# Receptance by seven products in one slot of four, states times std, the second norm's sums on ScalarE, and the next unit's attention first in a slot

## The chip, the cores and the metric

The kernel runs on one core of one Trainium2 chip, in float32 throughout. The metric is the device time of one execution in microseconds. In the text PE is TensorE, DVE is VectorE, ACT is ScalarE, POOL is GpSimd, and SP is the engine that issues most DMAs.

## What is computed

One transformer-like layer on x of 4 batches x 2048 tokens x 512 features. The parts that matter, cut from the reference (M = 64; `_layernorm` subtracts the mean and divides by the root of variance + 1e-5):

```python
h = _layernorm(x) * (1 + ca) + sa
x = x + ga * attention(h)
h = _layernorm(x) * (1 + cb) + sb
x = x + gb * ffn(h)

# attention(u): gates omega, zeta and F are products of u with 64 + 64 + 128 columns, then a scan over tokens
z_new = d_t * (S_t * z - DT * A_t * S_t * y) ; y_new = d_t * (DT * S_t * z + S_t * y) ; state = [z_new, y_new] + F_t
y = einsum('btn,dn->btd', states, C) + einsum('bte,de->btd', u, D_mat)

# ffn(x): x_prev is x moved by one token
xr = mu_r * x + (1 - mu_r) * x_prev ; xk = mu_k * x + (1 - mu_k) * x_prev
r = sigmoid(xr @ W_r.T) ; k = square(relu(xk @ W_k.T)) ; out = r * (k @ W_v.T)
```

The factors sa, ca, ga, sb, cb, gb come per batch from a small product of silu(c).

## The kernel before

**Tiling.** A unit is 256 tokens (W) of one batch: two tiles of 128 tokens (NT = 2). There are 32 units; unit i belongs to block s = i // 4 and batch b = i % 4. All matmuls are float32; a contraction over 512 features is 4 steps of 128. The norm's scale is folded into the weights: D's product runs on raw x with weights `dg` scaled per batch, and its result is multiplied by the token's r = 1/std afterwards.

**Classes.** `Gates` (`gts[j]`) makes a unit's scan inputs: `load`, `norm` (ACT sums with accumulators, L181 and L183, then POOL's power, L188), `send` (r to DRAM, L192), `spread` (r back as a row on all partitions, `bc`, L200), `project` (PE, tile `pg`, L221), `multiply` (DVE, L227), `deliver` (ACT, L242). `scan(s)` returns the DVE steps of a block's scan, each with an estimated cost in us; they go into the list `side`, and `take(budget)` runs steps from it until the budget is used up. Its last step `by_batch` copies the states on ACT (L377) and sends them to tile `y` by eight DMAs (L380). A `None` in the list is passed over by the next `take`.

`Finish` (`fin[i]`) does the rest of a unit. `attend` makes D's product `pd` (L424, 4 matmuls per tile), C's product `pc` (L449, one matmul), adds both to x on DVE (L430 and L463), takes bn_stats for the second norm (L125, L126), POOL powers (L471, L472), and the normalised `xn` on ACT (L475). `mix` transposes xn on PE (`pt`, L494) and forms the two mixtures with the previous token by ACT and DVE (L500, L503), with the key's sums (L546 to L549) between. `shift` adds a row to the next x on POOL (L417). `key_fast` computes the 512 x 512 x 256 product of W_k by Strassen's scheme in Winograd's form: seven products of halves, 28 matmuls of 128 columns (L562) in four rounds into two PSUM tiles `pm`, added up by DVE (L570 to L580), then Relu and Square on ACT (L583, L518). `receptance` is the plain product: 8 matmuls of 512 columns (L592), Sigmoid from PSUM (L594). `value` makes `pv` (L607), multiplies by r and adds x on DVE (L610, L611), and sends the rows out (L613).

**Order.** Every engine runs its instructions in the order in which the code gives them; the schedule is written by hand (`manual_schedule`). The loop at L1029 has one pass ("slot") per unit. For i >= 4, with at = i % 4:

```python
f.key_fast()
norm_send(i + 9)
take(a); ahead.attend(lambda: take(a2)); fetch("dg", i + 3); take(b_)
f.receptance()
ahead.mix(...); load_t, spread of unit i + 9; gates(i + 8)
f.value(lambda: take(c)); fetch("wv", i + 2)
```

where `ahead` is unit i + 1. The budgets are fixed for at = 0, 1; at = 2 takes shares of what is left; at = 3 starts with `take(100)`, and puts the next block's scan into `side` at its end, so it has no scan steps of its own. The first four slots have their own order. Before the loop a long set-up (L683 to L1006) makes weights per batch and runs block 0's scan.

PSUM pools: `ps1` one buffer (`pg`), `ps2` two buffers each of `pm` and `pt`, `ps3` three of `px`. SBUF pools p1, p2, p3 have one, two, three buffers per tag; the tag `soft` is in p1.

Of the kernel before, what the change touches and what calls it, by code (L numbers as in the profile page):

```python
# [21 lines left out]
P = 128  # L22
# [25 lines left out]
def adaln_layer_kernel(ctx: ExitStack, tc: tile.TileContext, x, x_t, c_t, wmod, w_gate, w_b, b_gate, b_f, c_mat, d_mat,  # L48
# [28 lines left out]
    rs = const.tile([P, B, T // P], F32, name="rs")  # L77
# [18 lines left out]
    pmean = const.tile([P, KC, 2 * B], F32, name="pmean")  # L96
# [51 lines left out]
    class Gates:  # L148


        def __init__(self, unit):
            self.u = unit
            self.r = rs[:, unit.b, unit.t0 // P : unit.t0 // P + NT]
# [8 lines left out]
        def norm_dve(self):  # L162
            tag = self.u.tag
            mv = p2.tile([P, NT, 2], F32, tag="mv", name=f"mv_a{tag}")
            for n in range(NT):
                tile_stats(self.xs[n], mv[:, n, :], f"a{tag}_{n}")
            var = p2.tile([P, NT], F32, tag="var", name=f"var_{tag}")
            nc.vector.tensor_scalar_add(var, mv[:, :, 1], EPS)
            nc.gpsimd.tensor_tensor(self.r, var, neg_half, ALU.pow)

        def norm(self, junk=False):
# [16 lines left out]
            nc.gpsimd.tensor_tensor(self.r, var, neg_half, ALU.pow)  # L188

        def send(self, queue=nc.sync):  # L190
            self.row = dram.tile([W], F32, tag=f"st{self.u.tag}", name=f"st_{self.u.tag}")
            queue.dma_start(self.row.rearrange("(n p) -> p n", p=P), self.r)  # L192
# [5 lines left out]
        def spread(self, queue=nc.sync):  # L198
            self.bc = p2.tile([P, W], F32, tag="bc", name=f"bc_{self.u.tag}")
            queue.dma_start(self.bc, self.row.unsqueeze(0).broadcast_to([P, W]))  # L200
# [43 lines left out]
    def scan(s):  # L244
# [125 lines left out]

        def by_batch():

            y_of[s] = p2.tile([P, B, W], F32, tag="y", name=f"y_{s}")
            for q in range(Q):
                t = [pre[:, i].rearrange("p l q c -> p (l q c)")[:, ts(q, W)] for i in range(2)]
                for i in range(2):
                    nc.scalar.copy(t[i].rearrange("p (c l) -> p l c", l=L), f[:, i, :, q, :])  # L377
                for r in range(2):
                    for i in range(2):
                        nc.sync.dma_start(y_of[s][ts(i, M), 2 * q + r, :], t[i][ts(r, M), :])  # L380
# [6 lines left out]
            + [(fall_start, 0.8)]  # L387
# [3 lines left out]
        return [(soften_act, 0), None] + steps + [None, (by_batch, 0)]  # L391

    class Finish:


        def __init__(self, unit):
            self.u, self.tag = unit, f"c{unit.tag}"


            self.fast = unit.s > 0  # L400
            self.at = unit.i % 2 if self.fast else unit.b
# [17 lines left out]
        def direct(self, n, room=(ps3, "px")):  # L419

            u = self.u
            pd = room[0].tile([P, D], F32, tag=room[1], name=f"pd_{self.tag}_{n}")
            for k in range(KC):
                nc.tensor.matmul(pd, self.h[:, k, ts(n, P)], dg[:, self.at, k, :], start=(k == 0), stop=(k == KC - 1))  # L424
            return pd

        def add_direct(self, n, pd):
            u, xt = self.u, self.x[:, n, :]
            r = rs[:, u.b, u.t0 // P + n : u.t0 // P + n + 1]
            nc.vector.scalar_tensor_tensor(xt, pd, r, xt, ALU.mult, ALU.add)  # L430
# [11 lines left out]
        def rows(self, n):  # L442

            return ps3.tile([P, D], F32, tag="px", name=f"pc_{self.tag}_{n}")

        def states(self, n, pc):

            u = self.u
            nc.tensor.matmul(pc, y_of[u.s][:, u.b, ts(n, P)], cg[:, u.b, :], start=True, stop=True)  # L449

        def attend(self, between):
            xt = self.x
            mv = p2.tile([P, NT, 2], F32, tag="mv", name=f"mv_{self.tag}")
            pcs = None
            if self.pd is not None:
                pcs = [self.rows(n) for n in range(NT)]
            for n in range(NT):
                pd = self.direct(n) if self.pd is None else None
                pc = pcs[n] if pcs else self.rows(n)
                self.states(n, pc)  # L460
                if pd is not None:
                    self.add_direct(n, pd)
                nc.vector.tensor_add(xt[:, n, :], xt[:, n, :], pc)  # L463
                tile_stats(xt[:, n, :], mv[:, n, :], f"{self.tag}_{n}")
                if n == 0:
                    between()
            rstd = p2.tile([P, NT], F32, tag="rstd", name=f"rstd_{self.tag}")
            nmr = p2.tile([P, NT], F32, tag="nmr", name=f"nmr_{self.tag}")
            nc.vector.tensor_scalar_add(rstd, mv[:, :, 1], EPS)
            nc.vector.tensor_scalar_mul(nmr, mv[:, :, 0], -1.0)  # L470
            nc.gpsimd.tensor_tensor(rstd, rstd, neg_half, ALU.pow)  # L471
            nc.gpsimd.tensor_tensor(nmr, nmr, rstd, ALU.mult)  # L472
            self.xn = p1.tile([P, NT, D], F32, tag="xn", name=f"xn_{self.tag}")
            for n in range(NT):
                nc.scalar.activation(  # L475
                    self.xn[:, n, :], xt[:, n, :], AF.Identity, bias=nmr[:, n : n + 1], scale=rstd[:, n : n + 1]
# [63 lines left out]
        def key_sums(self):  # L540
            (b00, b01), (b10, b11) = self.quarters = [
                [self.mixed[:, 1, 2 * k : 2 * k + 2, ts(t, P)] for t in range(2)] for k in range(2)
            ]
            half = dg[:, 3].rearrange("p k d -> p (k d)")[:, ts(self.u.i % 2, 2 * D)]
            t = self.sums = half.rearrange("p (i k w) -> p i k w", i=4, k=2)
            nc.vector.tensor_sub(t[:, 0], b01, b00)  # L546
            nc.vector.tensor_sub(t[:, 1], b11, t[:, 0])
            nc.vector.tensor_sub(t[:, 2], b11, b01)
            nc.vector.tensor_sub(t[:, 3], b10, t[:, 1])  # L549

        def key_fast(self):
            (b00, b01), (b10, b11) = self.quarters
            t, s = self.sums, key_weights
            act = self.act = p1.tile([P, KC, W], F32, tag="act", name=f"act_{self.tag}")
            (c00, c01), (c10, c11) = [[act[:, 2 * o : 2 * o + 2, ts(h, P)] for h in range(2)] for o in range(2)]

            def products(*pairs):
                pk = ps2.tile([P, 2, 2, P], F32, tag="pm", name=f"pk_{self.tag}")
                for n, (left, right) in enumerate(pairs):
                    for j in range(2):  # L560
                        for k in range(2):
                            nc.tensor.matmul(  # L562
                                pk[:, n, j, :], left[:, k, ts(j, P)], right[:, k, :], start=(k == 0), stop=(k == 1)
                            )
                return pk[:, 0], pk[:, 1]

            add = nc.vector.tensor_add
            x1, x2 = products((wk[:, 0:2, : D // 2], b00), (wk[:, 2:4, : D // 2], b10))
            copy = nc.scalar.copy if self.u.b else nc.vector.tensor_copy
# [5 lines left out]
            x7, x3 = products((s[:, 2], t[:, 2]), (s[:, 3], b11))  # L575
# [3 lines left out]
            x4, _ = products((wk[:, 2:4, D // 2 :], t[:, 3]))  # L579
            add(c10, c10, x4)  # L580
            for e in range(KC // 2):
                a = self.act[:, 2 * e : 2 * e + 2, :]
                nc.scalar.activation(a, a, AF.Relu)  # L583
                self.squares(e)

# [31 lines left out]
    key_weights = dg[:, 2].rearrange("p k d -> p (k d)").rearrange("p (i k o) -> p i k o", i=4, k=2)  # L617

    def make_key_weights():
        s = key_weights  # L620
        (a00, a01), (a10, a11) = [
            [wk[:, 2 * k : 2 * k + 2, ts(o, D // 2)] for k in range(2)] for o in range(2)
        ]
# [3 lines left out]
        nc.vector.tensor_sub(s[:, 3], a01, s[:, 1])  # L627

# [116 lines left out]

    def gate_cols(dst, pt, name):

        raw, sgn = (const.tile([P, KC, B], F32, name=f"{kind}{name}") for kind in ("raw", "sgn"))
# [114 lines left out]
    means = shared_means()  # L863
    gts[0].diagonal(cg[:, 0, :W])
# [5 lines left out]
    shared_weights(1, pws[0])  # L870
    gts[1].diagonal(cg[:, 1, :W])
# [6 lines left out]
    pws = [shared_product(3, means)]  # L878
    gts[2].diagonal(cg[:, 2, :W])
# [11 lines left out]
    for i in range(2):  # L891
        for k in range(KC):
            nc.tensor.matmul(pb[:, i, :], wraw[:, k, i, :], mod[:, SA, k, :], start=(k == 0), stop=(k == KC - 1))
    gts[3].diagonal(cg[:, 3, :W])
# [91 lines left out]
    d_scaled(2, pcas[0])  # L986
# [3 lines left out]
    fin[0].attend(lambda: None)  # L990
    d_scaled(3, pcas[1])
# [36 lines left out]

    for i, f in enumerate(fin):  # L1029
        at = i % B  # L1030
        ahead = fin[i + 1] if i + 1 < len(fin) else None
        if i < 4:
# [15 lines left out]
            if i == 2:  # L1048
                make_key_weights()
            ahead.attend(lambda: take(2))  # L1050
            turn(turn_v[i])
# [29 lines left out]
        else:  # L1081
# [6 lines left out]
            f.key_fast()  # L1088
            if i + 9 < len(gts):
                norm_send(i + 9)  # L1090
            if at == B - 2:
                left = sum(e[1] for e in side if e)
                a, a2, b_, c = 0.33 * left, 0.11 * left, 0.45 * left, 0.11 * left
            else:
                a, a2, b_, c = (3.6, 1.2, 5.5, 1.2) if at else (3.0, 0.0, 7.0, 1.2)
            take(a)
            if ahead:
                ahead.attend(lambda: take(a2))
            fetch("dg", i + 3)
            take(b_)  # L1100
            f.receptance()
# [56 lines left out]
```

## Time and profile before

| what | value |
|---|---|
| median of 3 runs (lowest, highest) | 1152.9 us (1152.21, 1157.6) |
| the profiled execution's own time | 1154.13 us |
| its span on the core | 1152.4 us |
| mean granted PE clock | 0.985 |
| DMA, mean over the span | 144 GB/s, queue 1 at 54.6% of 16 engines |
| receptance, L592 | 256 matmuls of 512 columns in 512 records, 227.6 us busy |
| DVE addition of C's product, L463 | 64, 687 ns each |
| DVE bn_stats L125, bn_aggr L126 | 64 of 695 ns, 64 of 182 ns |
| ACT copies of states, L377 | 32, 676 ns each |

The rows of the groups give line, engine, operation and tiles with partitions x elements, then the total busy time in us and the mean in ns of one, then the engine's idle time just before them and what ended it. Matmuls overlap, so the time that one takes is read from start to start. PEld is the weight load, which runs beside the matmul. In timelines a row is a run of like instructions: start, duration from the first start to the last end, and how many; a bracket tells of idle time before them.

### The profile page before, as it was taken

The numbers are of one execution on the slowest core, as the hardware profiler recorded it, in microseconds if no ns is written. First come the engines' busy times: TensorE is split into PE (matmuls) and PEld (weight loads), VectorE is DVE, ScalarE is ACT, GpSimd is POOL, SyncE is SP. The second block draws the span as 40 slices with busy tenths as digits, with TensorE's granted clock in tenths as the row PEclk, the third lists the DMA queues.
The fourth block names the chain that finished last, engine by engine and source line by source line (L and its number), as shares of the span: only waits on it lengthen the run. The fifth ranks groups of instructions, "written<-read, shape, count | busy, mean of one in ns | idle before, by whom it ended". The sixth has DMA issues, their size and how long they took to land.

```text
span 1152.4 us, 14032 instructions
## 1 busy us (share of the span) xinstructions
PE 1119.8 (97%) x4460; PEld 680.9 (59%) x4460; DVE 819.1 (71%) x2251; ACT 560.4 (49%) x1055; POOL 165.9 (14%) x317
## 2 busy tenths in 40 slices
PE   7899999999999999999999999999999999999998
PEld 4556566665565666655656666566566645555555
DVE  5897778458884787748886588847876588855553
ACT  1655775755535654455435644546444533333331
POOL 0222101111101111111011111110111111111110
PEclk8889899999999999999999999999999999999999
DMA  9893363445676656567667665676564423343211
GB/s 319 285 194 112 95 188 111 151 159 89 159 160 170 136 161 159 93 174 160 157 132 196 151 143 123 141 178 140 146 149 127 143 79 118 119 146 128 92 55 37
DMA packets 125601, 166.38 MB, mean 144 GB/s; under 512 B 15700, under 2 KB 88404, under 8 KB 117720
## 3 DMA queue, kind: packets, MB, share of 16 engines
q1 hardware_dynamic: 122520, 164.17, 54.6%
q10 hardware_dynamic: 2688, 0.79, 0.3%
q0 software_dynamic: 320, 0.53, 0.3%
q8 instruction: 35, 0.57, 0.2%
q14 instruction: 38, 0.31, 0.1%
HBM read 136.07 MB, written 25.20 MB: 140 GB/s over the span
## 4 chain that ended last, share of the span: by engine, by line
PE 81%; DVE 11%; ACT 3%; DMA 2%; issue 1%; POOL 1%; DVEq 0%; POOLq 0%; ACTq 0%
PE pv_c L607 17%; PE pd_c L424 15%; PE pr_c L592 15%; PE pk_c L562 14%; PE pg L221 9%; PE pc_c L449 4%; PE pt_c L494 2%; PE pk_c L527 2%; DVE x L463 1%; DVE stats_c L125 1%; DMA bc<-st 1%; DMA st<-rs 1%; DVE uv L365 1%; PE turn_d L814 1%; DVE x L430 1%
## 5 line engine op out<-in xcount | busy, mean ns | idle before, releaser
L424 PE MATMUL pd_c<-dg,xt 128*128 128x512 f32 x512 | 232.2, 597 | 0.0
L592 PE MATMUL pr_c<-wr,mixed_c 128*128 128x512 f32 x512 | 227.6, 598 | 0.4 <-DVE act_c L578 0.4
L607 PE MATMUL pv_c<-wvb,act_c 128*128 128x512 f32 (+1 forms) x528 | 225.5, 580 | 1.1 <-DVE r_c L610 1.1
L503 DVE SCALAR_TENSOR_TENSOR mixed_c<-pt_c,prev_f,mixed_c 128x255 f32<-128x255 f32 x256 | 115.9, 479 | 91.1 <-ACT mixed_c L500 88.4
L592 PEld LDWEIGHTS pr_c<-wr,mixed_c 128*128 128x128 f32 x512 | 98.0, 192 | 122.3 <-issue 120.1
L475 ACT ACTIVATE xn_c<-x,nmr_c,rstd_c 128x512 f32<-128x512 f32 x64 | 48.6, 806 | 244.5 <-POOL nmr_c L472 244.5
L607 PEld LDWEIGHTS pv_c<-wvb,act_c 128*128 128x128 f32 x528 | 99.3, 190 | 107.9 <-issue 102.8
L424 PEld LDWEIGHTS pd_c<-dg,xt 128*128 128x128 f32 x512 | 96.0, 192 | 108.7 <-issue 107.6
L500 ACT ACTIVATE mixed_c<-pt_c,mod,now_f 128x256 f32<-128x256 f32 x256 | 130.4, 561 | 56.2 <-DVE mixed_c L503 52.6
L221 PE MATMUL pg<-xt,wgb 128*128 128x256 f32 x448 | 102.6, 383 | 0.0
L583 ACT ACTIVATE act_c<-act_c 128x512 f32<-128x512 f32 x56 | 34.8, 621 | 115.2 <-DVE act_c L578 115.2
L221 PEld LDWEIGHTS pg<-xt,wgb 128*128 128x128 f32 x448 | 84.1, 193 | 10.6
L430 DVE SCALAR_TENSOR_TENSOR x<-pd_c,rs,x 128x512 f32<-128x512 f32 x64 | 47.2, 738 | 59.0 <-PE pd_c L424 59.0
L562 PE MATMUL pk_c<-dg 128*128 128x128 f32 x672 | 79.9, 275 | 1.4 <-DVE r_c L610 1.4
L562 PEld LDWEIGHTS pk_c<-dg 128*128 128x128 f32 x672 | 77.3, 192 | 1.8 <-DVE r_c L610 1.8
L610 DVE TENSOR_TENSOR r_c<-pv_c,r_c 128x512 f32<-128x512 f32 (+1 forms) x66 | 44.2, 669 | 40.4 <-PE pv_c L607 31.7
L417 POOL TENSOR_TENSOR x<-x,d 128x1024 f32<-128x1024 f32 x30 | 70.8, 2360 | 0.0
L449 PE MATMUL pc_c<-cg,y 128*128 128x512 f32 x128 | 65.0, 592 | 0.0
L471 POOL TENSOR_TENSOR rstd_c<-rstd_c,neg_half 128x2 f32<-128x2 f32 x32 | 25.4, 793 | 272.6 <-DVE nmr_c L470 272.6
L562 PEld LDWEIGHTS pk_c<-mixed_c,wk 128*128 128x128 f32 x448 | 53.8, 192 | 16.4 <-issue 10.2
L242 ACT ACTIVATE pre<-g,bias 64x256 f32<-64x256 f32 x56 | 41.6, 743 | 36.0 <-DVE g L227 29.2
L562 PE MATMUL pk_c<-mixed_c,wk 128*128 128x128 f32 x448 | 55.0, 276 | 1.6 <-POOL mixed_c L506 1.6
(218 smaller groups left out, 1467.8 us busy)
## 6 DMA issues: line engine op xcount, KB each, us to landing
dg<-dg SPq DMA_DIRECT2D x30, 1024.0 KB, 12.2
xt<-in_x_t_dram SPq DMA_DIRECT2D x116, 256.0 KB, 7.2
wvb<-wv SPq DMA_DIRECT2D x26, 1024.0 KB, 5.2
x<-in_x_dram SPq DMA_DIRECT2D x32, 512.0 KB, 6.2
out_dram<-r_c SPq DMA_DIRECT2D x62, 256.0 KB, 2.1
xs<-in_x_dram SPq DMA_DIRECT2D x54, 256.0 KB, 6.3
wvb<-in_wmod_dram SPq DMA_DIRECT2D x5, 1024.0 KB, 9.0
y<-pre SPq DMA_DIRECT2D x64, 64.0 KB, 2.0
```

The lines of the kernel that those rows point to most:

```text
L221: nc.tensor.matmul(self.pg[:, i, :], wgb[:, b, k, ts(i, P)], self.xt[:, k, :], start=(k == 0), stop=(k == KC - 1))
L417: engine.tensor_tensor(xt, xt, d0[:, self.u.b, :].unsqueeze(1).broadcast_to([P, NT, D]), ALU.add)
L424: nc.tensor.matmul(pd, self.h[:, k, ts(n, P)], dg[:, self.at, k, :], start=(k == 0), stop=(k == KC - 1))
L430: nc.vector.scalar_tensor_tensor(xt, pd, r, xt, ALU.mult, ALU.add)
L449: nc.tensor.matmul(pc, y_of[u.s][:, u.b, ts(n, P)], cg[:, u.b, :], start=True, stop=True)
L475: nc.scalar.activation(self.xn[:, n, :], xt[:, n, :], AF.Identity, bias=nmr[:, n : n + 1], scale=rstd[:, n : n + 1])
L500: nc.scalar.activation(m, pt, AF.Identity, bias=mod[:, SB, k, b : b + 1], scale=now_f[:, b, i, k : k + 1])
L503: nc.vector.scalar_tensor_tensor(m[:, 1:], pt[:, : W - 1], prev_f[:, b, i, k : k + 1], m[:, 1:], ALU.mult, ALU.add)
L562: nc.tensor.matmul(pk[:, n, j, :], left[:, k, ts(j, P)], right[:, k, :], start=(k == 0), stop=(k == 1))
L592: nc.tensor.matmul(pr, mixed[:, 0, k, ts(n, P)], wr[:, k, :], start=(k == 0), stop=(k == KC - 1))
L607: nc.tensor.matmul(pv[:, at], act[:, k, ts(n, P)], wvb[:, self.at, k, at], start=(k == 0), stop=(k == KC - 1))
L610: nc.vector.tensor_mul(r[:, at], pv[:, at], r[:, at])
```

## The change

1. **Receptance.** A new helper `seven` holds the four rounds of seven products that `key_fast` had. The key uses it as before, with the third round in `px` instead of `pm`. In units where `fast_r` holds (at = 3 in the loop's second part, and the last four units) the receptance uses it too, with the mixture's token quarters as weights and halves of `wr` (256 columns) as moving operand. Sums of W_r's quarters are made once (slot 3, into `wvb[:, 2]`), sums of the mixture's quarters per unit on DVE (into a half of `wvb[:, 3]`); Sigmoid then reads SBUF.
2. **States times std.** `Gates` also makes std = (variance + eps) * r on POOL, and `send` writes both rows. A new step `load_std`, ahead of `fall_start` in the scan, loads std as rows into the buffer `soft` by four DMAs; `by_batch` multiplies by it on DVE in place of the ACT copy. C's matmul then goes on adding into D's PSUM tile, and one DVE instruction adds both, times r, to x. Units 0 and 1, whose `pd` is made in set-up, keep separate tiles.
3. **Second norm.** From unit 3 on, mean and squared deviation come from two ACT passes with accumulators per tile; `normalize` is split off from `attend`.
4. **Order.** In the slots with at = 0, 1, 2 `attend` of the next unit stands ahead of the key, and `normalize` behind the key's first copy. In at = 3 key and activation come first, and `normalize` stands behind the first copy of the receptance. `norm_send` moves behind that too. The budgets are new.

The core of the diff:

```diff
-            queue.dma_start(self.row.rearrange("(n p) -> p n", p=P), self.r)
+            queue.dma_start(
+                self.rows.rearrange("i (n p) -> p (i n)", p=P),
+                rs[:, self.u.b, self.u.s].rearrange("p i n -> p (i n)"),
+            )
...
+        def load_std():
+            t = env["std"] = place(p1, "soft", "std", Q * W, Q * W)
+            for b in range(B):
+                row = gts[s * B + b].rows[1:2, :]
+                nc.sync.dma_start(t[(b % 2) * M : (b % 2) * M + M, ts(b // 2, W)], row.broadcast_to([M, W]))
...
-                    nc.scalar.copy(t[i].rearrange("p (c l) -> p l c", l=L), f[:, i, :, q, :])
+                    nc.vector.tensor_mul(t[i].rearrange("p (c l) -> p l c", l=L), f[:, i, :, q, :], std)
...
+                    pd = self.direct(n, stop=False)
+                    self.states(n, pd, False)
+                self.add_direct(n, pd)
...
-                nc.vector.tensor_add(xt[:, n, :], xt[:, n, :], pc)
-                tile_stats(xt[:, n, :], mv[:, n, :], f"{self.tag}_{n}")
...
+            nc.scalar.activation(junk, x, AF.Identity, scale=-1.0 / D, accum_out=mean)
+            nc.scalar.activation(junk, x, AF.Square, bias=mean, accum_out=self.var[:, n : n + 1])
...
+            x7, x3 = products((s[:, 2], t[:, 2]), (s[:, 3], b11), room=(ps3, "px"))
...
+        def receptance_fast(self, then):
+            def copy(dst, src):
+                nc.scalar.copy(dst, src)
+                then()
+            self.r = [p2.tile([P, D], F32, tag="r", name=f"r_{self.tag}_{n}") for n in range(NT)]
+            self.seven(
+                list(zip(*self.token_quarters(0))), self.r_sums, quarters_of(wr), receptance_weights,
+                [[r[:, ts(o, D // 2)] for o in range(2)] for r in self.r], "r", copy,
+            )
+            for r in self.r:
+                nc.scalar.activation(r, r, AF.Sigmoid)
...
+    SHARES = ((0.0, 0.0, 7.0, 1.2, 0.0), (2.0, 1.2, 5.5, 1.2, 0.0)), (0.2, 0.1, 0.5, 0.1, 0.1)
...
+            late = at == B - 1
+            if late:
+                f.key_fast()
+                f.activate()
+            if fast_r:
+                f.receptance_sums()
+            second_norm()
+            if not late:
+                f.key_fast(ahead)
+            def then():
+                if late and ahead:
+                    ahead.normalize()
+                if not late:
+                    f.activate()
+                if i + 9 < len(gts):
+                    norm_send(i + 9)
             take(b_)
-            f.receptance()
+            if fast_r:
+                f.receptance_fast(then)
+            else:
+                then()
+                f.receptance()
+            take(d_)
```

## The prediction

> **What bounds the kernel now.** I read the busy rows first, then the chain that ended last, then each loop pass on TensorE (PE), then the waits that stop it.
>
> ```profile
> PE 1119.8 (97%) x4460; PEld 680.9 (59%) x4460; DVE 819.1 (71%) x2251; ACT 560.4 (49%) x1055; POOL 165.9 (14%) x317
> ...
> PE 81%; DVE 11%; ACT 3%; DMA 2%; issue 1%; POOL 1%; DVEq 0%; POOLq 0%; ACTq 0%
> ```
>
> A busy PE need not be a full PE, so I take one pass of the loop (i = 16, at = 0) from the PE timeline and look at start times:
>
> ```profile
> 649.22 1.95 PE L562 MATMUL pk_c<-mixed_c,wk 128*128 128x128 f32 x16
> ...
> 655.47 3.60 PE L424 MATMUL pd_c<-dg,xt 128*128 128x512 f32 x8
> 658.91 1.02 PE L449 MATMUL pc_c<-cg,y 128*128 128x512 f32 x2
> 659.77 3.60 PE L424 MATMUL pd_c<-dg,xt 128*128 128x512 f32 x8
> 663.20 1.02 PE L449 MATMUL pc_c<-cg,y 128*128 128x512 f32 x2
> 664.06 7.03 PE L592 MATMUL pr_c<-wr,mixed_c 128*128 128x512 f32 x16
> 670.92 1.04 PE L494 MATMUL pt_c<-ident,xn_c 128*128 128x128 f32 x8
> 671.80 3.62 PE L221 MATMUL pg<-xt,wgb 128*128 128x256 f32 x16
> 675.25 7.03 PE L607 MATMUL pv_c<-wvb,act_c 128*128 128x512 f32 x16
> ```
>
> Start to start: key 6.25, the block of pd and pc 8.59, pr 6.86, pt 0.88, pg 3.45, pv 6.87 (the next key starts at 682.12): 32.90 us, and no row has an idle mark. (A matmul leaves two records, so x16 is 8 matmuls.) The granted clock is 1.00 in this stretch. PE is therefore full, and a pass gets shorter only by PE work removed. What stops PE elsewhere stands in the list of waits (total us, times, longest):
>
> ```profile
> PE pt_c L494 <- ACT xn_c L475: 4.9, 14, 1.1
> ```
>
> One of these waits on the PE timeline, in pass 14 (at = 2):
>
> ```profile
> 604.48 0.33 PE L494 MATMUL pt_c<-ident,xn_c 128*128 128x128 f32 x1 [0.19 <-ACT xn_c L475]
> 605.18 0.98 PE L494 MATMUL pt_c<-ident,xn_c 128*128 128x128 f32 x7 [0.37 <-ACT xn_c L475]
> ```
>
> In the passes with at = 2 the second norm comes late, because VectorE (DVE) carries most of the scan there. From start times, pr to pt has 0.36 too much and the first transpose 0.60: 0.95 us, in five such passes (338, 471, 604, 737, 869 us). Passes 24 to 26 have no gates (29.5 us long) but a scan, and DVE is the chain: the gaps on PE from 943 to 1008 us sum to 4.7 us. The first 136 us hold some 41 us of gaps and half clock, in set-up and pass 0. Nothing else is left.
>
> **Receptance by seven products.** Units 7, 11, 15, 19, 23, 27 and 28 to 31 (ten) change. Each loses 8 matmuls of 512 columns and gains 14 of 256: seven products of a 256-wide half, two contraction steps each. By rows: 8 of 512 take 6.87 us, 0.859 each. 8 of 256 (L221) take 3.45, 0.431 each. 14 x 0.431 = 6.04. Gain 0.83 per unit, **8.3 us** in ten.
>
> Here a rule of the Trainium skill speaks against it. TensorE: Matmul & The Clock Gate, section "Back-to-back issue gap", has the spacing of a stream set by weight load and matmul together, 81 ns where streaming alone gives 56 at 128 columns: shorter matmuls pay more. I take the difference, 25 ns, on every record (an estimate from that page). A unit has 28 records after and 16 before, so 12 x 25 = 0.3 us more: the gain would be 0.53 per unit, 5.3 in all. L221's row has 0.431 against half of 0.859, 0.002 apart, with weight loads of 193 ns hidden under it. I take the row.
>
> Beside it DVE gets 4 sums (0.42 back to back 0.35, rows L546 to L549) and 7 adds of 0.42 (L571 to L580) per unit, about 4.5 us, and ACT one copy (0.37). They lie in passes without scan steps (at = 3, and the last four): in the at = 3 pass from 616 us DVE is busy for 16.0 of 32.9 us. Rounds of four products last 1.72 us on PE and ask at most 3 x 0.42 = 1.26 of DVE. Hidden. Without that cover: 4.5 x 10 = 45 us.
>
> **C's product onto D's.** PE work is the same (64 products). DVE loses 64 additions (L463, 0.687; 44.0), gains 4 of 0.738 in units 0 and 1. Two px tiles per pass fall away. Added: 28+4 sends of twice the elements, a POOL product of 128x2 (L472's 0.25) each, 32 loads of std on SP, and in by_batch 32 DVE products in place of 32 ACT copies. No row shows a strided DVE product of this shape: nearest are 0.42 (L571, same size) and ACT's own 0.676 (L377, same strides). I take 0.45, 1.8 us per scan; at 0.68 it is 2.7. The sends land in 8.9 us (the DMA issues' row). If twice the elements cost nothing, as I take it, nothing moves; if they cost twice as long, bc goes out 9 us later and still has most of a pass. The std loads (64 KB each, as y<-pre, which lands in 2.0) stand on SP in the at = 2 pass behind the second load of xs, whose buffer comes free at about 20 us of the pass (below); by_batch wants them at 32.6.
>
> **Second norm by ScalarE.** DVE loses 58 x (0.695 + 0.182) and 29 x 0.33 = 60.5 us. ACT gains 58 pairs; the same pair in the first norm (L181, L183) runs 0.61 + 0.70, so 76 us. POOL gains 29 x 0.2. In all, DVE: -44 + 3 - 60 + 14 + 10 x 4.5 + 3 (weight sums) = about -39 us; ACT: 560 + 76 + 4 - 22 = 618. Both stay under PE, so none of this is a gain in itself; it counts where DVE is the chain.
>
> **Order in a slot.** In at = 0, 1, 2 PE now runs attend, key, receptance, transposes, and xn has from about 15 us to 21.7 us into the pass, where it had none to spare. (Tile 1 of pd is done at 8.6, its addition at 9.4, key's first product and copy at 9.9, two sums 1.3, POOL 1.3, two xn 1.5: 14 to 15.) The five waits of 0.95 go: **-4.8**. Attend at the head needs dg, x_t and y a third of a pass earlier; they were asked for a pass before and land in 7 to 12 us. SP's second load of xs now waits for the first norm at 20 us of the pass instead of 10, and behind it stand dg, st, x_t, bc; the tightest of them, bc, has a pass left.
>
> In at = 3 xn must be ready when the fast receptance ends. From attend's end: copy at 0.9 to 1.3, sums of tile 1 to 2.6, POOL 1.3, two xn 1.5, so 5.4 against 6.04. It fits by 0.6. Queued on ACT behind those two waits (for DVE and for POOL) are the first norm (3.4 us) and the two sigmoids, so the next mix begins at 25 us of the pass instead of 22; the pass after starts with attend, so its key wants that mix at 32.1 + 8.6: covered by 9 us.
>
> **What is late next.** The key of at = 3 still comes first, right behind a pass in which DVE does the rest of the scan. There: last key add at 15.5 us of the pass, seven state steps of 1.2 (23.9), one more (25.1), mix and key sums 5.4 (30.5), gates 0.7, pv's first pair 1.4 (32.6), by_batch 1.8 (34.4), second product 0.7 (35.1). The key's second round needs that PSUM tile at 32.95 + 1.79 = 34.74. So PE waits 0.4 in five passes: **+2.2**; at 0.68 per product 1.3 each, +6.5; at best nothing. Before pass 27, without the gates' 3.45, the second product ends at 34.4 and the second round would start at 29.5 + 1.8: a wait of 3.1, in place of the 4.7 above: **-1.6**. The 0.54 ahead of the last receptance (its tile now comes from the other pool) goes: **-0.5**. Set-up: SP now waits with the std loads for the buffer "soft" until about 50 us, and the load of wm_sb behind them goes out at 52 instead of 41.9; it is wanted at 60.2 and lands in 5 to 9, so 0 to +1. POOL's products ahead of the DMA chain of pass 0 add 0.3. I take **+0.5**. A gain there isn't excluded: ACT loses 2 us of copies ahead of a norm.
>
> **Sum.** -8.3 - 4.8 + 2.2 - 1.6 - 0.5 + 0.5 = -12.5 on a span of 1152.4, so 1139.9. The profiled run took 1154.1, 1.7 more than its span; the median shown is 1152.9, 1.2 below it. Off the median: 1140.4. I say **1141**.
>
> **Rivals.**
> A. *The wait moves to at = 3.* The chain to xn fits by only 0.6, and by_batch may cost 0.68. If the chain runs 0.5 too long in six passes and the key waits 1.3 in five: +3 + 4.3 on 1141, 1148. For it: ACT, DVE and POOL hand over five times. Against: each link is a measured row.
> B. *The shorter matmuls pay*, as the rule has it: 3 us less gain, 1144. With all 120 additional weight loads exposed (0.192 each) it would be 23 less, 1164, but L221 exposes none of its own, so I give that end no weight.
> C. *Slower: DVE reaches the key late in at = 1 and 2.* Scan steps now stand ahead of key's adds, and round 4 wants round 1's PSUM tile 3.5 us after it is full. By my sum DVE is there on time: value's last pair ends at 1.4 us of the pass, two steps of 1.9 at 5.2, first addition 6.0, a step 7.9, second addition at 9.4, and round 1 is full at 10.4. With a lag of 4.5 behind round 1, PE would wait 1.04 in each of 12 passes and the 12.5 are gone; from 5.0 on it is slower by more than 0.5%; a lag of 6 gives 12 x 2.5 = 30, 1171. For it: DVE is busy 27.8 of 32.9 us in such a pass now (from 682 us). Against: 3.5 of that go.
> D. *Set-up loses.* wm_sb lands after 60.2, 1 us late, and the PE gaps that follow bring the half clock back twice. Once costs 2.5 us: the receptance at 119.9 us takes 9.41 on the chain in place of 6.87. Together +6, 1147.
>
> **Chances.** Forecast (1136 to 1145) 0.60; A 0.18; B 0.06; C 0.09; D 0.07. About 0.5%, 5.8 us, is what can be told from no change here. Faster by more than that (below 1147.1): the forecast 0.60, B 0.06, half of D 0.035, 0.4 of A 0.07, in all 0.76. Slower: nearly all of C, 0.08. Within: the rest, 0.16. Range: at the low end no new wait at all and the gaps of 943 to 1008 us gone wholly, a further 2.2 + 3.1, 1135; the high end takes in A with its dear half and D, 1150. Left out are C, A's dear end and a little below.
>
> **What would show it.** Right: pr in two shapes, 256-wide at 0.431 start to start; no wait of pt on xn in at = 2; PE slots of 32.1 us in at = 3; DVE near 780, ACT near 620. Wrong: in at = 3 a mark of pt waiting for xn, in key's second round of DVE's r_c, or in at = 1 and 2 any idle before key's fourth round.

## The result, and the profile after

The changed kernel takes 1167.61 us (median of 4 runs, 1163.49 to 1170.83); the kernel before took 1155.18 beside it on the same chip (4 runs). The ratio is 1.0107, 95% interval 1.006 to 1.0154: slower by about 12 us, where 12 less were forecast. The profiled execution took 1163.49 us, with a span of 1161.7.

The busy row and the chain that ended last, from the page of the changed kernel:

```profile
PE 1110.6 (96%) x4580; PEld 703.0 (61%) x4580; DVE 783.7 (67%) x2163; ACT 635.8 (55%) x1265; POOL 178.3 (15%) x378
...
PE 75%; DVE 10%; DMA 7%; ACT 4%; issue 2%; POOL 1%; SPq 1%; DVEq 0%; POOLq 0%; ACTq 0%
```

PE is busy for 9.2 us less and DVE for 35 less, near what was forecast (8.3 and 39). The new thing is DMA: 7% of the chain where it had 2%. The chain between 20 and 70 us (start, us, what) says which:

```profile
21.91 18.26 DMA wvb<-in_wmod_dram
40.17 0.02 issue
40.19 23.52 DMA xs<-in_x_dram
63.70 0.02 issue
63.73 0.77 ACT xs L182 x3
```

Two loads of the set-up take 18.3 and 23.5 us. ACT waits for the second, and behind its norm stands the copy row_gb, for which PE waits 9.2 us. I compare where slot 4 begins: at 251.27 us before, at 268.97 after. What follows takes 901.1 us before and 892.7 after. So the loop gains 8.4 us, and the set-up with the first four slots loses 17.7.

Now SP's own timeline in the set-up, after:

```profile
21.91 0.83 SPq L726 DMA_DIRECT2D wvb<-in_wmod_dram  x1
22.86 4.56 SPq L194 DMA_DIRECT2D st<-rs  x3
27.52 3.29 SPq L726 DMA_DIRECT2D wvb<-in_wmod_dram  x1
30.86 1.75 SPq L733 DMA_DIRECT2D room<-in_c_mat_dram  x1
32.71 0.46 SPq L726 DMA_DIRECT2D wvb<-in_wmod_dram  x1
33.26 1.41 SPq L194 DMA_DIRECT2D st<-rs  x1
40.19 9.81 SPq L159 DMA_DIRECT2D xs<-in_x_dram  x2
...
52.88 10.83 SPq L381 DMA_DIRECT2D std<-st  x4
63.81 0.53 SPq L726 DMA_DIRECT2D wvb<-in_wmod_dram  x1
```

and the same part of before:

```profile
22.67 2.58 SPq L658 DMA_DIRECT2D room<-in_c_mat_dram  x1
27.18 0.37 SPq L651 DMA_DIRECT2D wvb<-in_wmod_dram  x1
27.59 5.36 SPq L159 DMA_DIRECT2D xs<-in_x_dram  x2
...
41.86 0.37 SPq L651 DMA_DIRECT2D wvb<-in_wmod_dram  x1
```

Four sends of the norms (L194) now stand among the loads. The load of xs goes out 12.6 us later, and the last row of each fence, wm_sb, 22 us later. What the DMA engines do meanwhile is in the DMA view of 22 to 45 us, 40 slices of 0.575 us. After:

```profile
DMA  9999999999999999999859093392574499496682
GB/s 288 315 346 392 374 388 385 392 392 378 388 395 406 406 420 270 74 94 15 7 21 64 0 39 14 25 43 25 61 46 46 61 57 36 43 75 53 32 39 18
...
st<-rs SPq DMA_DIRECT2D x4, 2.0 KB, 30.0
```

and before:

```profile
GB/s 302 317 378 385 392 392 385 378 388 392 395 406 402 420 378 367 406 410 400 381 369 403 404 407 415 406 406 399 406 417 392 399 399 402 399 410 328 171 338 410
```

From 31 us on the engines are busy for most of the time and move 0 to 94 GB/s in place of about 400. A send of 2 KB, 512 packets of four bytes, lands after 30 us (the median of four). The records of that stretch show which packets take the time: between 30 and 35 us 1,600 packets of 4 bytes at 10 ns each, and the loads' packets of 2 KB at 287 ns in the mean, later 450 to 560, where before they took 84 to 92. The slow stretch is longer than this view. Over 15 to 80 us, in slices of 1.625 us, the changed kernel shows:

```profile
GB/s 333 362 368 297 300 366 389 387 398 351 62 30 21 29 45 55 49 44 43 50 54 171 338 396 313 73 48 60 166 217 325 403 303 298 388 355 122 45 41 69
```

The rate is down from 31 to 49 us, though from 33 to 50 us only one four-byte packet starts. It is down again from 55.6 us, right behind the last send, with some 560 four-byte packets between 53 and 56 us. So the slow stretch outlasts the records of the small packets, the first time by some 16 us.

The granted PE clock follows. From 45 to 70 us PE is busy for 8.0 us of 25 (21.8 before), and from 70 to 105 us the granted clock is 0.84 where it was 1.00 before. With PE busy for 33.6 of these 35 us I estimate that about 5 us of the loss (0.16 x 33.6) is the slower clock.

### The profile page after: what moved, and what is told of

The parts are those of the page before. It is cut to its first block, busy times and chain, and to the rows that moved or that the text cites. A ratio compares the mean times of both kernels' runs of the same rounds, so it can differ in the third digit from the quotient of the medians.

```text
span 1161.7 us, 14452 instructions
## 1 busy us (share of the span) xinstructions
PE 1110.6 (96%) x4580; PEld 703.0 (61%) x4580; DVE 783.7 (67%) x2163; ACT 635.8 (55%) x1265; POOL 178.3 (15%) x378
## 4 chain that ended last, share of the span: by engine, by line
PE 75%; DVE 10%; DMA 7%; ACT 4%; issue 2%; POOL 1%; SPq 1%; DVEq 0%; POOLq 0%; ACTq 0%
PE pd_c L438 18%; PE pv_c L671 15%; PE pk_c L583 14%; PE pr_c L656 10%; PE pg L226 6%; PE pd_c L461 4%; PE pr_c L583 3%; DMA xs<-in_x_dram 2%; PE pt_c L523 2%; PE pk_c L556 2%; DMA wvb<-in_wmod_dram 2%; DVE uv L370 1%; DVE pre L390 1%; DVE mixed_c L532 1%; DMA x<-in_x_dram 1%
## 5 line engine op out<-in xcount | busy, mean ns | idle before, releaser
L656 PE MATMUL pr_c<-wr,mixed_c 128*128 128x512 f32 x352 | 156.7, 598 | 0.0
L490 ACT ACTIVATE xn_c<-x 128x512 f32<-128x512 f32 x58 | 36.5, 630 | 141.0 <-DVE x L446 141.0
L656 PEld LDWEIGHTS pr_c<-wr,mixed_c 128*128 128x128 f32 x352 | 66.1, 193 | 75.0 <-issue 73.0
L503 ACT ACTIVATE xn_c<-x,mean_c,var_c 128x512 f32<-128x512 f32 x64 | 48.6, 806 | 61.3 <-POOL mean_c L501 61.3
L499 POOL TENSOR_SCALAR var_c<-var_c 128x2 f32<-128x2 f32 x29 | 5.6, 191 | 431.6 <-ACT xn_c L491 431.6
L461 PE MATMUL pd_c<-cg,y 128*128 128x512 f32 x120 | 61.3, 592 | 0.0
```

The source lines that it names most:

```text
L503: nc.scalar.activation(self.xn[:, n, :], self.x[:, n, :], AF.Identity, bias=self.mean[:, n : n + 1], scale=self.var[:, n : n + 1],)
L656: nc.tensor.matmul(pr, mixed[:, 0, k, ts(n, P)], wr[:, k, :], start=(k == 0), stop=(k == KC - 1))
```

## The experiments

There are two theories for the 17.7 us. **Elements**: the sends' four-byte packets hold up the loads beside them. **Order**: SP runs in order, and its waits, for the norms ahead of the sends and for the room and the rows ahead of block 0's std loads, delay the loads behind. A third says that it isn't in the set-up but in the first slots.

**The sends alone, in the kernel before.** Nothing of the change but this (a norm's two values come from two POOL products):

```python
+ t = dram.tile([2 * W], ...)                       # for units 0 to 3, at the places of send()
+ nc.sync.dma_start(t.rearrange("(n p) -> p n", p=P), rs2[:, b])
```

> The kernel before, with four writes added that nothing reads: at the four places where the changed kernel sends the first norms, 512 four-byte elements each go to DRAM on SP's queue, from two POOL products more per unit. Theory 1 (elements: 2,048 four-byte writes hold the DMA engines while the set-up's loads wait beside them): +14 to +18 us, so 1169 to 1173, and 2 KB packets of 300 to 500 ns between 30 and 50 us in place of 84 to 92. Theory 2 (order: only SP's waits for the norms, and the wait of the std loads that this kernel has not, cost time): the four sends' own waits and issues, about 6 us of SP of which loads in flight hide some, so +2 to +5 us.

Measured: 1169.1 us, ratio 1.0119 (1.0096 to 1.0143). Four writes that nobody reads cost 14 us: more than the 12 by which the changed kernel is slower, and most of the 17.7. The DMA view of 22 to 45 us shows the same collapse, and from 70 to 105 us the granted clock is 0.84 here too:

```profile
GB/s 295 313 353 388 392 378 392 385 388 392 381 395 410 413 424 231 116 176 68 39 36 14 21 43 32 43 28 61 25 18 25 18 50 32 32 25 64 93 82 36
...
wo<-rs SPq DMA_DIRECT2D x4, 2.0 KB, 22.7
```

**The same bytes in 16-byte packets**: `"(p n) -> p n"` in that rearrangement, so that a partition's four values are neighbours in DRAM.

> As the run before in this list (kernel before plus four writes that nothing reads, at the same places and with the same waits), but each partition's four values lie side by side in DRAM, so each send is 128 packets of 16 bytes and not 512 of 4 bytes. Theory 1 (the number of elements costs): a quarter of the other run's loss, +3 to +5 us. Theory 2 (order and waits on SP cost): the same loss as the other run.

Measured: 1154.04 us, ratio 0.9988 (0.9971 to 1.0006). The loss is gone, though SP still waits for the same norms at the same places. So it isn't the waits for the norms that cost; the std loads, the other half of "order", are not in this kernel.

**The same four-byte packets, 64 bytes apart.** The tile is `[2 * W, 16]` and the write goes to its first column.

> The kernel before, with four writes of 512 four-byte elements that nothing reads, as in the first of these runs (1169.1 us), but each element 64 bytes from the next in DRAM. If the number of packets costs: the same loss, +15 us, 1169. If it costs that 16 neighbouring elements lie in one stretch of 64 bytes and are written by different DMA engines: little, +0 to +4 us, 1154 to 1158.

Measured: 1153.11 us, ratio 0.9996 (0.9984 to 1.0007). As many packets, of the same size, cost nothing that can be told from the noise, and the granted clock from 70 to 105 us is 1.00 again. The rate in the DMA view dips for some seven slices, four us, and comes back, and a send lands after 10.4 us in place of 22.7:

```profile
GB/s 300 330 385 385 370 399 385 395 385 374 395 399 427 388 350 92 45 50 25 211 164 224 349 349 370 339 368 408 406 406 361 354 371 413 406 410 413 395 399 406
...
wo<-rs SPq DMA_DIRECT2D x4, 2.0 KB, 10.4
```

So my theory needs a correction: it isn't the number of four-byte packets, but that they lie side by side. No distance other than 64 bytes was tried, and with it a write also spreads over 32 KB of DRAM in place of 2.

**The changed kernel without block 0's std loads.**

```python
  t = env["std"] = place(p1, "soft", "std", Q * W, Q * W)
+ if s == 0:
+     nc.vector.memset(t, 1.0)
+     return
```

> The changed kernel, without the four loads of std for block 0: a constant 1.0 is written by VectorE in their place, so block 0's outputs lack that factor; the four early sends stay. Theory 1 (elements of the sends): the loads of before 50 us still crawl, so only part of SP's 10.83 us returns: -1 to -4 us, 1163 to 1167. Theory 2 (SP stands for 10.83 us before the weights of shift b and what follows): -9 to -11 us, 1157.

Measured: 1160.42 us, ratio 1.0051 (1.0037 to 1.0066). By the ratios that is 6.5 us less than the changed kernel, though the two intervals overlap a little: more than "elements" gave, less than "order". The list of SP's waits in the changed kernel (us in total, times, longest) fits, because most of SP's 10.83 us at the std loads is a wait for a send:

```profile
SPq L381 <- DMA st<-rs: 6.5, 1, 6.5
```

**Block 0's std spread by TensorE**, as the reciprocals are, without early sends and std loads:

```python
+ nc.gpsimd.tensor_tensor(diag_std[:, ts(n, P)], ident, std[:, n : n + 1].broadcast_to([P, P]), ALU.mult)
...
+ nc.tensor.matmul(pt[h : h + M, ...], ones[:, :M], gts[b].diag_std[:, ts(n, P)], start=True, stop=True)
+ nc.scalar.copy(t, pt)
...
- gts[0].send()   # and 1, 2, 3
```

> The changed kernel with block 0's std spread by TensorE as the reciprocals are (POOL makes eight more diagonals, eight 128-column products with ones, one copy by ScalarE), so that the four early sends and the four std loads of block 0 are not there. Theories 1 and 2 both: the set-up's 16 to 18 us return, slot 4 begins at 251 to 254 us, and the time is 1148 to 1153. Theory 3 (the loss lies in the first slots themselves: VectorE's products, the new waits): the set-up is shorter by up to 16 us at 66 us, but slot 4 begins no earlier than 260, and the time stays above 1158.

Measured: 1149.42 us (12 runs, 1145.45 to 1156.79), ratio 0.9953 (0.9932 to 0.9974). Slot 4 begins at 253.6 us, against 251.27 before and 268.97 with the sends. The third theory falls for all but some 2 us.

**The changed kernel with 8-byte packets.** Sends and std loads stay. A row of norms lies in DRAM by partition, and `multiply` and `by_batch` read it with a stride:

```python
- self.rows.rearrange("i (n p) -> p (i n)", p=P)
+ self.rows.rearrange("i (p n) -> p i n", p=P)
...
+ self.bc = self.bc.rearrange("q (p n) -> q n p", n=NT)
```

> The changed kernel with its early sends and std loads kept, but every row of norms lies in DRAM by partition, so that each send is 256 packets of 8 bytes in place of 512 of 4; the readers take the values with a stride. Theory 1 as a count of packets (half as many): half of the sends' loss, 1159 to 1161. Theory 1 as a matter of size (16 bytes cost nothing, so 8 may too): the sends' loss of some 11 us returns whole and the std loads' stays, 1154 to 1157. Rival (packets don't matter here but the wait for the norms does): 1167.

Measured: 1140.04 us (1139.3 to 1142.05), ratio 0.989 (0.9875 to 0.9905). All of the loss is gone and more: a layout of 2 KB rows is worth 25 us by the ratios. In the profiles the first key comes 15.9 us earlier than in the changed kernel (105.7 us against 121.6), and slot 0, from key to key, is 7.7 us shorter (31.6 against 39.3). The sends are not free in this form: the rate between 22 and 45 us still falls to between 118 and 249 GB/s for about 6 us.

```profile
GB/s 300 339 367 388 381 388 385 385 388 385 392 410 424 381 323 277 390 229 118 140 154 179 183 165 185 143 129 249 304 364 377 399 366 399 389 395 395 278 36 46
```

The excess over my expectation suggested that the kernel before loses to its own sends too.

**The kernel before with 8-byte packets**, the same edit and nothing else.

> The kernel before, with nothing of the change, but every row of norms in DRAM by partition, so that each of its 28 sends is 128 packets of 8 bytes in place of 256 of 4 (the 8-byte form gave 1140.0 us with the change in). Theory 1 (neighbouring 4-byte packets hold up loads wherever a send meets them): in the kernel before this costs slot 0, which lasts 36.96 us from key to key there and 31.55 in the changed kernel with 8-byte packets, so -5.4 us, 1148; the rest of those 13 us is the change's own. Rival (the kernel before, whose sends come later, loses nothing to them): 0 +- 1 us, and the change alone is worth 13.

Measured: 1149.1 us, ratio 0.9968 (0.9957 to 0.9978): 3.7 us less, where I expected 5.4. In slot 0 PE's turn of the value weights waits less on DVE's addition, which stands behind a product that waits for `bc`. The list of waits, first before, then this run:

```profile
PE turn_v L814 <- DVE x L463: 2.8, 2, 1.9
```

```profile
PE turn_v L817 <- DVE x L466: 0.9, 1, 0.9
```

First key to second key takes 36.96 us before and 32.01 here. The shorter waits are 1.9 of these 5 us. Another 2.6 are the receptance behind them: 9.45 us from its start to that of the transposes before, 6.87 here. The granted clock says why: from 119.7 to 124 us it is 0.50 before and 1.00 here. The row before and the row here:

```profile
119.71 9.62 PE L592 MATMUL pr_c<-wr,mixed_c 128*128 128x512 f32 x16
```

```profile
117.49 7.03 PE L595 MATMUL pr_c<-wr,mixed_c 128*128 128x512 f32 x16
```

So the change itself, with 8-byte sends in both kernels, is worth 0.989 / 0.9968 = 0.992, some 9 us.

**The std loads, with 8-byte packets**: the edit of the constant 1.0 again.

> The changed kernel with 8-byte packets (1140.0 us) and without block 0's four std loads: VectorE writes a constant 1.0 in their place, so block 0's outputs lack that factor. With the 4-byte packets the same edit gave 7.2 us. Theory (the std loads cost only because SP waited there for a send that the crowd held up): 0 to -1 us, 1139 to 1140. Rival (SP's wait for the room and for the rows delays the weights of shift b by itself): -4 to -7 us, 1133 to 1136.

Measured: 1138.62 us, ratio 0.9876 (0.9862 to 0.9889), by the ratios 1.6 us less than with the loads, the intervals overlapping. SP's wait in itself costs little; beside the four-byte sends the same edit was worth 6.5.

**Plain receptance**, on the version with std by TensorE:

```python
- fast_r = at in FAST or i >= len(fin) - B
+ fast_r = False
```

> The version with block 0's std spread by TensorE (measured at 1149.4 us), with the receptance as two plain products of four in all slots. Theory 1 (the seven products give what their TensorE time says, 0.83 us in each of ten units, and a wait of 0.56 us in five last slots takes 2.8 us of it back, because ScalarE's second norm then stands behind the shorter work): +8.3 - 2.8 = +5.5 us, 1155, TensorE busy for 8.3 us longer, no wait ahead of the transposes in the last slots. Rival (the seven products give nothing in the last slots, and the remaining gain is from the states product and the norm): 0 to +1 us.

Measured: 1150.38 us, ratio 0.9965 (0.9948 to 0.9983), against 0.9953 with the seven products: by these times alone, nothing. From the start of slot 4 to the end it takes 896.1 us against 892.5, so 3.6 us are there, of the 5.5 expected; in the medians the scatter between runs (1145.45 to 1156.79 with the seven products) hides them. The wait ahead of the transposes isn't there, as expected.

**ScalarE's sums ahead of its copy**, on the same version:

```python
  def copy(dst, src):
+     first()                    # ahead.stats(NT - 1), when at = 3
      nc.scalar.copy(dst, src)
      then()                     # normalize, without those sums
```

> The version with block 0's std spread by TensorE (1149.4 us), and in the last slot of four ScalarE takes the second row's sums before it copies the receptance's first product, and not after. Theory 1 (the wait of 0.56 us ahead of the transposes is xn's, one copy of 0.37 us and a wait for the product too late): xn lands about 1.0 us earlier, the wait goes in five passes, -2.8 us, 1146.6. Rival (the copy's 0.9 us delay runs through VectorE's seven sums into the last one of r and so into the product's room on PSUM): the wait moves there, 0 to +2 us.

Measured: 1142.76 us, ratio 0.9902 (0.9889 to 0.9914). From slot 4 on it takes 888.8 us, 3.7 less than without the edit; six waits of 0.56 are 3.4. Beside it, plain receptance, which has no such wait either, takes 7.3 us longer from slot 4 on, and 7.6 by the medians of one chip: this pair is the price of the receptance, forecast at 8.3.

**Both repairs**: 8-byte packets and the sums ahead.

> The changed kernel with 8-byte packets (1140.0 us) and with ScalarE's sums of the second row ahead of its copy of the receptance's first product in the last slot of four. Theory: five waits of 0.56 us go, -2.8 us, 1137.2. Rival (with the loads free, xn is not what these five waits end on): 0 us.

Measured: 1138.16 us (1136.15 to 1138.45), ratio 0.9868 (0.9855 to 0.9882), the fastest of all; against 8-byte packets alone the intervals overlap, so the second repair's 2.8 us is not shown by the times. From slot 4 on it takes 888.5 us against 892.2. In this execution the first key came at 108.5 us and not 105.7, which ate the difference in the span. The mark ahead of pt is gone (PE, pass with at = 3):

```profile
498.92 1.03 PE L589 MATMUL pr_c<-wvb,mixed_c 128*128 128x256 f32 x4
499.79 1.04 PE L529 MATMUL pt_c<-ident,xn_c 128*128 128x128 f32 x8
```

## Why the prediction was wrong, by its own steps

**The step that failed** is the set-up's, "I take +0.5". It priced one load, wm_sb, behind the std loads (out 10 us later; measured 22), and a POOL product. Of the sends it said, under C's product, "If twice the elements cost nothing, as I take it, nothing moves", counted "28+4" of them and looked for who waits for `bc` in the loop. The four were new in the set-up, ahead of loads that wait for nobody, and there the 8.9 us of a send in the loop is no price. By the ratios, 1.0107 against 0.989, the layout of the sends costs the changed kernel 25 us, of which the kernel before paid 3.7 too. By the profiled spans the forecast was short by 21.8 us: 17.2 of them lie ahead of slot 4 (+17.7 for +0.5), 4.6 from slot 4 on (-8.4 for -13.0). Rival D named the place and the half clock, and priced them at +6; the sends it did not name.

**Receptance, -8.3: right.** A pass with at = 3 on PE, after:

```profile
499.90 1.95 PE L583 MATMUL pk_c<-mixed_c,wk 128*128 128x128 f32 x16
502.19 2.94 PE L583 MATMUL pk_c<-dg 128*128 128x128 f32 x24 [0.34 <-DVE r_c L674]
...
515.35 1.89 PE L583 MATMUL pr_c<-wr,mixed_c 128*128 128x256 f32 x8
517.07 2.75 PE L583 MATMUL pr_c<-wvb 128*128 128x256 f32 x12
519.66 1.03 PE L583 MATMUL pr_c<-wr,wvb 128*128 128x256 f32 x4
520.52 1.03 PE L583 MATMUL pr_c<-wvb,mixed_c 128*128 128x256 f32 x4
521.39 0.29 PE L523 MATMUL pt_c<-ident,xn_c 128*128 128x128 f32 x1
522.06 0.98 PE L523 MATMUL pt_c<-ident,xn_c 128*128 128x128 f32 x7 [0.38 <-ACT xn_c L503]
```

515.35 to 521.39 is 6.04 us, the forecast to the digit, and no idle mark stands inside. The row was right, and the rule of the weight loads (rival B) would have given 6.34.

**xn in at = 2, -4.8: right.** No pass with at = 2 has a mark ahead of its transposes, as in this one:

```profile
481.84 7.03 PE L656 MATMUL pr_c<-wr,mixed_c 128*128 128x512 f32 x16
488.71 1.04 PE L523 MATMUL pt_c<-ident,xn_c 128*128 128x128 f32 x8
```

**"It fits by 0.6" in at = 3: wrong by 1.2.** The last two rows of the pass above show the wait, 0.56 by start times, in six passes, 3.4 us: half of rival A. ACT's rows of the pass say why:

```profile
517.27 0.37 ACT L639 COPY r_c<-pr_c 128x256 f32<-128x256 f32 x1 [3.60 <-PE pr_c L583]
517.54 0.63 ACT L490 ACTIVATE xn_c<-x 128x512 f32<-128x512 f32 x1
518.07 0.19 ACT L490 ACTIVATION_READ_ACCUMULATOR xn_c<-x 128x1 f32 x1
518.30 0.72 ACT L491 ACTIVATE xn_c<-x,mean_c 128x512 f32<-128x512 f32 x1
518.92 0.19 ACT L491 ACTIVATION_READ_ACCUMULATOR xn_c<-x,mean_c 128x1 f32 x1
520.49 1.52 ACT L503 ACTIVATE xn_c<-x,mean_c,var_c 128x512 f32<-128x512 f32 x2 [1.37 <-POOL mean_c L501]
```

The copy starts 1.92 us after 515.35, not 0.9: it waits for both products of the first round, four matmuls of 0.43, not for one. That shift is the 1.0. Every sum also carries a row of its own that reads the accumulator (0.19), so that tile 1's two sums take 1.57 and not 1.3. Over the whole kernel these rows of the second norm are 21.7 us; ACT is busy for 635.8, where 618 was forecast.

**Key's second round in at = 3, +2.2: right, a little low.** 0.6 us in four passes and 0.85 in the first (0.50 to 0.74 and 0.10 behind it), 3.3 in all. A term that was mis-sized is by_batch:

```profile
L390 DVE TENSOR_TENSOR pre<-f,std 128x256 f32<-128x256 f32 x32 | 18.1, 631 | 0.0
```

0.63 us is the mean of one, nearer to the upper of the two ends (0.68) than to 0.45. Back to back the four ahead of the second product take 2.27 us, where 1.8 was forecast. The wait grew by less than that 0.47, because they began earlier than the sum had it: in this pass value's first pair ends at 499.34, 32.34 us after the pass before began, and not at 32.6.

**Passes 24 to 31, -1.6 and -0.5: too much.** PE's gaps from 924 us on sum to 7.3 us before and 6.5 after, so about -0.7. In pass 27 the waits are 3.4 where 3.1 was forecast; the last receptance lost its 0.54, but a key of the last slot waits 0.70 for r, which the sum did not have.

**Rival C, at 1171, has the right time and the wrong cause**: in at = 1 and 2 no pass of the loop has an idle mark ahead of key's fourth round.

From slot 4 on the steps add up to -8.3 - 4.8 + 3.3 + 2.8 (five of the six waits in at = 3 passes; the sixth is in pass 27's share) - 0.7 = -7.7 against -8.4 in the profile, where -13.0 was forecast.

## What to carry to other kernels

A DMA that the kernel already has is not a price for the same DMA at another place: ask which loads are under way when it runs, and how its packets lie in DRAM. A row of norms written with the partition as the fastest index made four-byte neighbours. In this kernel the layout cost 25 us, for sends of 2 KB each; with the same row by partition, read with a stride, that loss was gone. And where a chain across engines "fits by 0.6", list its first wait exactly: which record releases it, and what stands ahead of it on its engine.

## What the runs showed of the hardware

Four writes of 512 four-byte packets, side by side in DRAM, cost 14 us in the kernel before. In the changed kernel 1,600 such packets held the core's DMA rate under 95 GB/s for some 18 us, 16 of them after the last had started. The same packets 64 bytes apart cost nothing that can be told from the noise (0.9996), nor did packets of 16 bytes side by side (0.9988). Packets of 8 bytes lie between in the DMA view: 118 to 249 GB/s for about 6 us.

The packets' own records don't show it: 9 to 10 ns each in all of these runs. It shows in the 2 KB packets of the loads. Between 34 and 42 us their mean was 1.08 us in the kernel before with four-byte neighbours and 0.54 in the changed kernel, against 0.087 with the packets 64 bytes apart. Part of the cost, some 5 us by the estimate above, is the granted PE clock: 0.84 from 70 to 105 us in these two kernels, 1.00 before and with the packets 64 bytes apart.

The Trainium skill (DMA: Bandwidth & Descriptors, section "Specifications") names 512 bytes as the least transfer for full rate, with read-modify-write below; these runs agree that small packets slow the loads, and show that the size alone doesn't set the price, since 4 bytes were free 64 bytes apart. Why neighbours cost more, and whether the page's read-modify-write has to do with it, no run here shows; whether they cost as much with no load beside them was not tried.
